# Unread matrix products in TensorE's holes, and a later place for part of a combine

## The chip, the cores and the metric

The kernel runs on one core of a Trainium2 chip. A core has five engines that run side by side, each with its own instruction queue taken in order: TensorE (PE, matrix products; its weight loads are listed as PEld), VectorE (DVE), ScalarE (ACT), GpSimd (POOL) and SyncE (SP, which here only issues DMAs). Products land in PSUM, eight banks, and are copied out by VectorE or ScalarE. The metric is the device time of one launch in microseconds (us), the median of three runs.

## The reference

Two layers on x of shape (2, 1024, 256), all float32. Layer 0: an adapter with layer norm and an RWKV-like recurrence, then a conditional feed-forward `cond2` whose output goes into a mixture of experts. Layer 1: a sparse attention `cond`, a windowed attention with side blocks, an adapter and a feed-forward. The change touches the part from `cond2` to the end of the sparse attention:

```python
h  = gelu(x @ W1 + b1); c2 = concat(h @ W2 + b2, h @ We[idx] + be)   # hidden width 1024
probs = softmax(c2 @ Wg); vals, idx = top_k(probs, 2)                # 8 experts
keep  = (one_hot == 1) & (position_in_expert < 512)                  # first choices first
x = x + sum_e combine[:, e] * (gelu(c2 @ W1[e] + b1[e]) @ W2[e] + b2[e])
Q, K, V = x @ Wq.T + bq, x @ Wk.T + bk, x @ Wv.T + bv                # 16 heads of 16
s = (Q K^T) / 4 at 32 gathered keys of each query; out = softmax(s) V @ Wo.T + bo
```

The keys that a query gathers are counted per key, and the logarithm of the count is added to dense scores over the first 256 keys, which is the same sum.

## The kernel before

The residual `x` stays in SBUF, channels on partitions, as two halves of 128 channels by 2048 tokens. The program is written with a tile framework: it finds the dependences between tiles, sets the semaphores, and orders each engine's instructions when the kernel is built, by program order as a priority and by its own costs. An instruction that is ready in that plan may be issued ahead of one written earlier.

**`cond2_0` and `Route`.** Tokens are taken in five chunks of 4, 4, 4, 3 and 1 blocks of 128 (`C2CK`). Of each chunk, eight hidden slices are made (line 671, Gelu at 674), then two halves of the output (line 680, copied out at 687). `choose` then makes router scores and the two chosen experts of each token. `place` counts tokens per expert with small products against a triangle and ones (lines 800 and 804), makes each token's slot (`si`, line 820) and issues one indirect DMA per block and choice from POOL (line 823), which scatters the token's row into a DRAM table `xs` by expert. The placing of chunk n-1 stands behind the hidden slices of chunk n, so that it has something to hide behind; that of chunk 3 stands behind the first output half of chunk 4, and that of chunk 4 at the end. `finish` makes the combine weights `cw` (softmax from line 863, Exp at 864) and, from a count over all tokens (line 841, copied at 843), the mask `k.more`.

**`moe`.** Eight experts, 512 slots each. For each one, two tables are loaded (`xe`, `more`, line 963; for expert 0 in four pieces), merged on VectorE (line 967), turned by eight 128x128 transposes on TensorE into two banks `pt` (line 982), one for each half of the channels, and copied by ScalarE to `xt` (line 983). 16 products of 512 columns follow (line 988, Gelu at 991), then 32 of 256 columns (line 996), bias on VectorE (line 999), and an indirect DMA back to `ys` from POOL (line 1000). A float32 product is two instructions in the trace, a transpose is one. Beside the first four experts VectorE counts keys (line 918), 32 instructions for each of eight query blocks.

**`combine` and `cond1_near`.** `combine` loads the two expert rows of each token for four chunks of 512 tokens (line 1029) and returns, for each chunk, three steps: `weighed` (VectorE scales and adds, lines 1038 and 1039) and two `add` steps (four transposes at line 1045, an addition to `x` at 1046). `cond1_project` gives a list of steps for one batch row: queries in four products of 512 tokens, keys, values. Before the middle attention begins, chunks 0 and 1, the whole projection of row 0, and the `weighed` steps of chunks 2 and 3 are done. Then 32 items follow (row, pair of query blocks, group of four heads): `scores` (line 1229), `weights` in two halves (VectorE adds the log counts and finds the maximum, line 1245; ScalarE's Exp at 1255), `turn` (transposes at 1264, copies at 1268), `values` (line 1292). Three items are in work at a time. What is still missing, the rest of the combine, row 1's projection and later each item's division (lines 1164 to 1176) and the output products (line 1191), waits in a first-in first-out list `later`. Each item takes one step from it ahead of `values`, and a second one behind `weights` if more than four wait. All of them share one PSUM bank. What is left in the list after the last item is run off at the end.

## Time and profile before

| | us |
|---|---|
| median of three runs | 1513.05 |
| the three runs | 1504.31, 1513.05, 1513.1 |
| the profiled execution | 1505.63 |
| its span, first to last instruction | 1503.6 |
| TensorE busy in the span | 1418.2 |
| VectorE busy | 875.4 |
| ScalarE busy | 682.6 |
| GpSimd busy | 207.4 |
| mean granted TensorE clock | 0.962 of full speed |

The page gives for each engine its busy time; busy TensorE is modelled and pipelined, so 94% is not 94% of its peak. PEclk is the clock that the throttle granted to TensorE, as a share of full speed. In the timeline, a row is a run of equal instructions: start, time, engine, line, operation, out<-in, count, and in brackets how long the engine sat idle before it and what ended that. The stretches that this document speaks of, in us from the span's start: routing to 402, the experts from 402 to 642, the combine and the projections to 669, the middle attention to 860, and the windowed attention and the last feed-forward behind it.

### The profile page before, as it was taken

How to read it: one execution, taken by the hardware profiler on the slowest of the kernel's cores; microseconds unless marked ns; L12 is line 12 of the kernel's file. 1: busy time of each engine (PE TensorE's matmuls, PEld its weight loads, DVE VectorE, ACT ScalarE, POOL GpSimd, SP SyncE). 2: the span in 40 equal slices, each digit the busy share in tenths (PEclk: the TensorE clock that was granted, in tenths of full speed). 3: DMA queues.
4: the chain of work that ended last, by engine and by line, in shares of the span. 5: the costliest groups of instructions: out<-in, count | busy, mean ns of one | idle time of the engine just before them, and what ended most of it. 6: DMA issues, size and time to landing. Idle time of an engine off the chain costs nothing. (4 is left out here: it accounts for less than half of the span.)

```text
span 1503.6 us, 27351 instructions
## 1 busy us (share of the span) xinstructions
PE 1418.2 (94%) x10788; PEld 966.2 (64%) x10788; DVE 875.4 (58%) x2775; ACT 682.6 (45%) x1683; POOL 207.4 (14%) x165
## 2 busy tenths in 40 slices
PE   6998889999699999979999999999999999999998
PEld 3446876445466766745666545788886457878866
DVE  5455643111599911067887703887883247778764
ACT  3433332322222123127888621765674337656733
POOL 3343620022311811100000000000001000000011
PEclk9899688999799999989999999999999999999999
DMA  9500004201433342030000010000000000000001
GB/s 309 189 1 3 4 9 165 108 30 38 128 118 128 119 153 71 21 119 2 2 1 2 29 56 0 2 2 2 2 2 1 0 0 2 2 1 2 2 14 44
DMA packets 42758, 70.77 MB, mean 47 GB/s; under 512 B 7168, under 2 KB 35840, under 8 KB 39552
## 3 DMA queue, kind: packets, MB, share of 16 engines
q1 hardware_dynamic: 36576, 57.12, 11.3%
q0 software_dynamic: 3072, 8.65, 1.6%
q10 hardware_dynamic: 2976, 3.18, 0.7%
q8 instruction: 87, 1.43, 0.4%
q14 instruction: 47, 0.39, 0.1%
HBM read 45.09 MB, written 23.86 MB: 46 GB/s over the span
## 5 line engine op out<-in xcount | busy, mean ns | idle before, releaser
L1643 ACT ACTIVATE pe<-pe,nm 128x320 f32<-128x320 f32 x256 | 141.8, 555 | 131.2 <-DVE nm L1633 131.0
L1633 DVE CUSTOM_DVE_ANT_0 pe<-ps,wbs 128x320 f32<-128x320 f32 x256 | 118.6, 487 | 6.1 <-PE ps L1627 1.8
L1255 ACT ACTIVATE pe<-pe,nm 128x256 f32<-128x256 f32 x256 | 110.5, 498 | 19.6 <-DVE nm L1245 19.5
L988 PE MATMUL ph<-xt,w 128*128 128x512 f32 x256 | 114.0, 603 | 2.2 <-ACT xt L983 2.2
L1623 PE MATMUL ps<-kT,qT 64*128 64x384 f32 (+1 forms) x512 | 110.2, 498 | 3.3 <-DVE qT L1597 2.8
L996 PE MATMUL po<-w,h 128*128 128x256 f32 x512 | 111.8, 379 | 0.0
L996 PEld LDWEIGHTS po<-w,h 128*128 128x128 f32 x512 | 97.3, 190 | 16.6 <-issue 3.8
L1245 DVE CUSTOM_DVE_ANT_0 pe<-ps,lc 128x256 f32<-128x256 f32 x256 | 94.1, 417 | 19.1 <-PE ps L1229 18.3
L1692 PE MATMUL py<-ptt,v 128*64 128x128 f32 x1408 | 103.6, 277 | 0.1
L918 DVE SCALAR_TENSOR_TENSOR lc<-iok,idx,lc 128x256 f32<-128x256 f32 x248 | 100.1, 479 | 0.0
L988 PEld LDWEIGHTS ph<-xt,w 128*128 128x128 f32 x256 | 48.6, 193 | 62.2 <-issue 55.6
L1000 POOL DMA_INDIRECT ys<-ye,row x32 | 60.8, 1899 | 182.3 <-DVE ye L999 162.8
L1692 PEld LDWEIGHTS py<-ptt,v 128*64 128x64 f32 x1408 | 78.6, 137 | 11.3 <-issue 8.3
L1665 PE MATMUL pt<-ident,pe 128*128 128x128 f32 x512 | 79.8, 282 | 1.9 <-DVE pe L1651 0.9
L1264 PE MATMUL ptp<-ident,pe 128*128 128x128 f32 x512 | 73.0, 280 | 3.7 <-DVE pt L1268 3.7
L991 ACT ACTIVATE h<-ph,vecs 128x512 f32<-128x512 f32 x64 | 44.0, 687 | 69.2 <-PE ph L988 69.2
L1264 PEld LDWEIGHTS ptp<-ident,pe 128*128 128x128 f32 x512 | 55.3, 141 | 31.0 <-ACT pe L1255 14.8
L1652 ACT ACTIVATE pe<-pe,rd 128x320 f32<-128x320 f32 x128 | 70.7, 557 | 8.9 <-DVE rd L1650 8.9
L1627 PEld LDWEIGHTS ps<-sk,qT 64*128 64x128 f32 x512 | 50.9, 187 | 26.2 <-issue 0.3
L1672 DVE TENSOR_TENSOR ptt<-pt,tri 128x512 f32<-128x512 f32 x96 | 65.0, 677 | 0.0
L1665 PEld LDWEIGHTS pt<-ident,pe 128*128 128x128 f32 x512 | 56.1, 140 | 10.9 <-issue 2.0
L999 DVE TENSOR_TENSOR ye<-po,b 128x256 f32<-128x256 f32 x32 | 13.5, 422 | 79.5 <-PE po L996 79.5
(368 smaller groups left out, 2784.0 us busy)
## 6 DMA issues: line engine op xcount, KB each, us to landing
w<-in_mw SPq DMA_DIRECT2D x16, 1024.0 KB, 5.2
xs<-z SPq DMA_DIRECT2D x8, 1088.0 KB, 11.7
ys<-z SPq DMA_DIRECT2D x4, 1024.0 KB, 11.4
xe<-xs SPq DMA_DIRECT2D x7, 544.0 KB, 7.0
more<-xs SPq DMA_DIRECT2D x7, 544.0 KB, 4.1
out_x<-o SPq DMA_DIRECT2D x8, 256.0 KB, 2.2
x<-in_xT SPq DMA_DIRECT2D x3, 512.0 KB, 6.4
wa<-in_wa SPq DMA_DIRECT2D x1, 1536.0 KB, 8.1
```

The costliest lines, as they stand in the source:

```text
L918: nc.vector.scalar_tensor_tensor(n, key, k.idx[:, qb, j : j + 1], n, ALU.is_equal, ALU.add)
L988: nc.tensor.matmul(ph, lhsT=w1[:, c, m * P : (m + 1) * P], rhs=xt[:, c, :], start=c == 0, stop=c == 1)
L996: nc.tensor.matmul(po, lhsT=h[:, m, j * P : (j + 1) * P], rhs=w2[:, m, :], start=m == 0, stop=m == 7)
L1245: nc.vector.tensor_tensor_reduce(out=pe[:, j, :], in0=it["ps"][i][:, j, :], in1=k.lc[:, q0 + j, :], scale=-1.0, scalar=3.0e38, op0=ALU.add ...
L1255: nc.scalar.activation(pe[:, j, :], pe[:, j, :], AF.Exp, bias=nm, scale=-1.0)
L1264: nc.tensor.transpose(ptp[:, kb, j, :], it["pe"][i][:, j, kb * P : (kb + 1) * P], k.ident)
L1623: nc.tensor.matmul(ps[:, i, keys[i]], lhsT=qs[i], rhs=kT[hp, m + pair, k0 : k0 + nk], start=True, stop=True)
L1633: nc.vector.tensor_tensor_reduce(out=pe[:, i], in0=ps[:, i, used[i]], in1=wbs[:, 0 if n == 0 else 3 if n == NB - 1 else 1 + i, (1 - i) * G ...
L1643: nc.scalar.activation(pe[:, i], pe[:, i], AF.Exp, bias=nm[:, i : i + 1], scale=-1.0, accum_out=den[:, i : i + 1])
L1652: nc.scalar.activation(pe[:, 1], pe[:, 1], AF.Copy, scale=rd[:, 1:2])
L1665: nc.tensor.transpose(pt[1 - j if i and inner(n) else j][:, 2 * pair + i, :], pe[:, at : at + P], k.ident)
L1692: nc.tensor.matmul(py[64 * i : 64 * i + 64, (m + pair) % 4, :], lhsT=keys[:, hs], rhs=it["pts"][:, pair, :] if j == 3 else it["pt"][:, j, ...
```

## The change

Three helpers of order and filling come in. `behind` adds an edge of order without a semaphore, so that one instruction is issued behind another on its engine. `spin` issues products of the identity with itself into a bank that nobody reads, each behind the one before, 512 columns unless told otherwise. `k.step`, `k.placed` and `k.added` remember the instruction to stand behind.

- `cond2_0`: `place(ch - 1)` stands ahead of both output halves for every chunk, so for the last one too.
- `finish`: its first VectorE instructions, the copy of the count and the subtraction ahead of Exp, stand behind the last slot of `place`.
- `moe`: seven spins for expert 0 behind the count; both `pt` banks are taken at once and the transposes go block by block, for every expert; with expert 0 a spin of 256 columns stands behind each of the first three blocks.
- `combine`: the scaling of chunks 1 to 3 stands behind the last addition or the last reduction of `weights` written before it; chunk 0's transposes stand behind the spins.
- `cond1_project`: for the near form, values come ahead of the queries of the row's second half.
- `cond1_near`: ahead of the items there are eight spins, chunk 0's three steps, two spins, and five projection steps (queries and keys of the first half, values). The list begins with chunk 1, the two other query steps of row 0, chunks 2 and 3 with their scalings, and row 1's projection. Two spins of 256 columns stand in the run-off at the end.

```diff
+def behind(k, ins, other):
+    how = mybir.DependencyInfo(mybir.DependencyClass.NoSync, mybir.DependencyReason.DATA)
+    k.tc.add_manual_dep(ins.ins, other.ins.name, how, reason="order")
+    return ins
+
+def spin(k, bank, other, count, n=4):
+    for _ in range(count):
+        rhs = k.ident.unsqueeze(1).to_broadcast([P, n, P])
+        out = bank[:, 0 : n * P].rearrange("p (n c) -> p n c", c=P)
+        other = behind(k, k.nc.tensor.matmul(out, lhsT=k.ident, rhs=rhs, start=True, stop=True), other)
+    return other
...
-            if 0 < ch < end:
+            if ch:
                 place(ch - 1)
...
-                if ch == end and c == 0:
-                    place(ch - 1)
             choose(ch)
-        place(end)
+        place(ch)
...
-        nc.vector.tensor_add(self.si[:, bs], q, at)
+        k.placed = nc.vector.tensor_add(self.si[:, bs], q, at)
...
-        nc.vector.tensor_copy(c1, pc[:, 0, 0])
+        behind(k, nc.vector.tensor_copy(c1, pc[:, 0, 0]), k.placed)
...
-        nc.vector.tensor_sub(ex, self.L, bc(self.top))
+        behind(k, nc.vector.tensor_sub(ex, self.L, bc(self.top)), k.placed)
...
+            pts = [pp.tile([P, CAP], F32, name="pt") for _ in range(2)]
+            if e == 0:
+                warm = pp.tile([P, 2 * C], F32, name="po", bufs=4)
+                k.step = spin(k, warm, k.step, 7)
+            for j in range(4):
+                for c in range(2):
+                    t = nc.tensor.transpose(pts[c][:, j * P : (j + 1) * P], xe[:, j, c * P : (c + 1) * P], k.ident)
+                    if e == 0:
+                        k.step = behind(k, t, k.step)
+                if e == 0 and j < 3:
+                    k.step = spin(k, warm, k.step, 1, 2)
             for c in range(2):
-                pt = pp.tile([P, CAP], F32, name="pt")
-                for j in range(4):
-                    nc.tensor.transpose(pt[:, j * P : (j + 1) * P], xe[:, j, c * P : (c + 1) * P], k.ident)
-                nc.scalar.copy(xt[:, c, :], pt)
+                nc.scalar.copy(xt[:, c, :], pts[c])
...
-            nc.vector.tensor_scalar_mul(o, o, k.cw[:, 0, blk : blk + 1])
+            first = nc.vector.tensor_scalar_mul(o, o, k.cw[:, 0, blk : blk + 1])
+            if ch:
+                behind(k, first, k.added)
...
-    return steps + [lambda bank, j=j: values(bank, j) for j in range(0, keys // P, 2)]
+    n = 4 if keys < S else len(steps)
+    return steps[:n] + [lambda bank, j=j: values(bank, j) for j in range(0, keys // P, 2)] + steps[n:]
...
-            for step in sums[0] + sums[1] + project[0] + [sums[2].pop(0), sums[3].pop(0)]:
+            warm = wp.tile([P, CK], F32, name="warm")
+            k.step = spin(k, warm, k.step, 8)
+            for step in sums[0]:
+                step(lambda shape: pp.tile(shape, F32, name="pb"))
+            k.step = spin(k, warm, k.step, 2)
+            for step in project[0][:5]:
                 step(lambda shape: pp.tile(shape, F32, name="pb"))
...
-            second = [lambda step=step: step(bank) for step in sums[2] + sums[3] + project[1]]
+            second = [lambda step=step: step(bank) for step in sums[1] + project[0][5:] + sums[2] + sums[3] + project[1]]
...
-            for step in later:
+            warm = None
+            for i, step in enumerate(later):
                 step()
+                if len(later) - i in (5, 3):
+                    warm = warm or bank([P, CK])
+                    k.step = spin(k, warm, k.step, 1, 2)
```

More of the change, by code (lines that the diff above doesn't have):

```diff
@@ L660, in cond2_0 @@
     ):
-        end = len(C2CK) - 1
         for ch, (b0, nb) in enumerate(C2CK):
@@ L840, in finish @@
         pc = self.pp.tile([P, CK // P, 2, E], F32, name="pc")
-        nc.tensor.matmul(pc[:, 0, 0], lhsT=k.ones, rhs=self.run[:, 0, 0], start=True, stop=True)
+        k.step = nc.tensor.matmul(pc[:, 0, 0], lhsT=k.ones, rhs=self.run[:, 0, 0], start=True, stop=True)
         c1 = rt.tile([P, E], F32, name="c1")
-        nc.vector.tensor_copy(c1, pc[:, 0, 0])
+        behind(k, nc.vector.tensor_copy(c1, pc[:, 0, 0]), k.placed)
         k.more = rp.tile([P, E, CAP // P], F32, name="more")
@@ L995, in moe @@
                 for m in range(8):
-                    nc.tensor.matmul(
+                    k.step = nc.tensor.matmul(
                         po, lhsT=h[:, m, j * P : (j + 1) * P], rhs=w2[:, m, :], start=m == 0, stop=m == 7
@@ L1044, in add @@
         for j in range(4):
-            nc.tensor.transpose(po[:, j * P : (j + 1) * P], gs[ch][0][:, j, c * P : (c + 1) * P], k.ident)
-        nc.vector.tensor_add(x[:, c, ts], x[:, c, ts], po)
+            t = nc.tensor.transpose(po[:, j * P : (j + 1) * P], gs[ch][0][:, j, c * P : (c + 1) * P], k.ident)
+            if ch == 0:
+                k.step = behind(k, t, k.step)
+        k.added = nc.vector.tensor_add(x[:, c, ts], x[:, c, ts], po)
     return [
@@ L1163, in divide @@
         for g in range(4):
-            nc.tensor.transpose(pa[:, g, :], aU[g], k.ident)
+            k.step = nc.tensor.transpose(pa[:, g, :], aU[g], k.ident)
         p4 = pa.rearrange("p g (r d) -> p (g r) d", d=32)
@@ L1173, in back @@
         for c in range(2):
-            nc.tensor.transpose(pb[:, c, :], a2[:, c * P : (c + 1) * P], k.ident)
+            k.step = nc.tensor.transpose(pb[:, c, :], a2[:, c * P : (c + 1) * P], k.ident)
         for c in range(2):
@@ L1214, in cond1_near @@
             its += [dict(at=(b, q0, g), qT=qT, kT=kT, v=v, aT=aT) for q0 in range(0, 8, 2) for g in range(4)]
-        with tiles(tc, name="l1a", bufs=6, space=PSUM) as pp:
-            for step in sums[0] + sums[1] + project[0] + [sums[2].pop(0), sums[3].pop(0)]:
+        with tiles(tc, name="l1a", bufs=6, space=PSUM) as pp, tiles(tc, name="l1w", bufs=1, space=PSUM) as wp:
+            warm = wp.tile([P, CK], F32, name="warm")
[4 more added lines that the diff above has]
+            for step in project[0][:5]:
                 step(lambda shape: pp.tile(shape, F32, name="pb"))
@@ L1244, in weights @@
                         nm = sp.tile([P, 1], F32, name="nm", bufs=4)
-                        nc.vector.tensor_tensor_reduce(
+                        k.added = nc.vector.tensor_tensor_reduce(
                             out=pe[:, j, :],
```

## The prediction

> **What bounds the kernel now.** I read the page first: 1503.6 us of span in a profiled execution of 1505.63 us, so 2.0 us lie around the span. TensorE is busy for 94% and leads the chain that ended last (PE 28%, DVE 10%, ACT 3%). The row PEclk is 9 or 8 nearly everywhere, so only short pieces of the run can win from a faster clock. Then I asked for busy time and granted clock in stretches of 3.41 us around the two holes of TensorE that the change fills (393 to 414, 643 to 660) and the end of the middle attention (858 to 864). The columns are the stretch, its length, busy time of PE, PEld, DVE, ACT and POOL, granted clock, DMA share and GB/s.

> ```profile
> 396.77:400.18 3.41, 0.00 (x0) 0.00 (x0) 3.31 (x26) 0.00 (x0) 2.50 (x4) 0.50 0.28 106
> ...
> 407.01:410.42 3.41, 2.18 (x7) 1.01 (x7) 2.46 (x9) 1.03 (x2) 0.00 (x0) 0.50 0.88 187
> 410.42:413.83 3.41, 3.41 (x5) 1.35 (x5) 3.31 (x10) 1.32 (x2) 0.00 (x0) 0.50 1.11 367
> ...
> 649.36:652.77 3.41, 2.37 (x8) 1.30 (x8) 2.08 (x6) 0.00 (x0) 0.00 (x0) 0.50 1.09 353
> ...
> 857.58:860.99 3.41, 2.08 (x15) 1.30 (x12) 2.30 (x9) 0.37 (x1) 0.00 (x0) 1.00 0.02 5
> 860.99:864.40 3.41, 3.41 (x5) 1.35 (x4) 2.57 (x5) 0.19 (x1) 0.00 (x0) 0.50 0.00 0
> ```

> The clock changes at the edges of such stretches. It falls to 0.50 after one with 2.08 us of products and comes back after one that is full. With 2.37 or 2.18 us at the low clock it doesn't come back. What the low clock costs is small: half of the 3.8 us in which expert 0's products ran slow (410.03 to 413.83), some 1.8 us in front of the attention, 1.7 us behind it.

> **Part 1, routing.** Now `place(3)` stands behind eight pairs of output products; this is the timeline.

> ```profile
> 386.10 1.95 PE L680 MATMUL po<-h,c2w 128*128 128x128 f32 x16
> 387.89 0.32 PE L800 MATMUL pc<-oh,tri 128*128 128x48 f32 x2
> ...
> 389.86 0.17 DVE L820 TENSOR_TENSOR si<-q,at 128x6 int32<-128x6 f32 x1
> ...
> 390.77 0.96 POOL L823 DMA_INDIRECT xs<-ct,si  x1 [8.65 <-issue]
> ...
> 399.72 0.96 POOL L823 DMA_INDIRECT xs<-ct,si  x1 [0.30 <-issue]
> ...
> 402.29 1.76 SPq L963 DMA_DIRECT2D xe<-xs  x4
> ```

> In front of both halves its counting starts at 386.10, 1.79 us earlier, and so does POOL's run of scatters, one each 1.27 us. The last two need the last block's `si`. Now it ends at 396.68; without `ex` (0.2) and the copy of `c1` with its wait for TensorE (0.26) in front it is ready at about 396.1, and POOL takes it some 0.75 us later, at 396.85 instead of 398.45. So the loads of `xe` start 1.6 us earlier (bounds 1.0 and 1.8). `finish` loses nothing: `ex` and its chain, 3.6 us of VectorE, then end near 401.3, before the first `xe` is there (405.07 less 1.6). POOL has no other work there, and SP's loads only wait for the scatters.

> **Part 2, the seven spins.** One is a 128x512 product, two instructions of 0.43 us at full clock (L988's step) and of 0.86 at half. From 396.0 they run 12.0 us if the clock stays low and about 8.1 if it is back at 400.18, so to 404.1, when the first `xe` is there. In 403.59:407.01 the rest of them, three short spins of 0.43 and six transposes (0.27 each) give 2.6 us of products, above the 2.08 that was followed by a fall. So I take it that expert 0 starts at full clock: 2.0 us of its 32 instructions (15.7 us instead of 13.66 at 0.427) are saved. [...]

> With 1.6 and 2.0 and 0.2 for faster transposes TensorE is 3.8 us ahead at expert 0's end, but VectorE, which counts keys (0.39 us x 32, twice per expert) without a break, is only 1.9 ahead (1.6, and 0.3 of a wait at 429.0 that goes). It ended expert 1's `xe` at 438.85, now 436.95; the last two transposes and a copy take 1.0 more, so L988 starts at 437.95 instead of 440.82: 2.9 us of the 3.8 arrive.

> **Part 3, the transposes of all experts.** The order changes from channel half by channel half to block by block. Where TensorE ends one expert and goes on, the copy to `xt` waits for the fourth transpose; afterwards for the seventh.

> ```profile
> 439.55 1.04 PE L982 MATMUL pt<-ident,xe 128*128 128x128 f32 x8
> ...
> 440.18 1.07 ACT L983 COPY xt<-pt 128x512 f32<-128x512 f32 x2 [13.56 <-PE pt L982]
> ...
> 440.82 1.98 PE L988 MATMUL ph<-xt,w 128*128 128x512 f32 x4 [0.24 <-ACT xt L983]
> ```

> Eight take 1.04 us, so they follow each other by 0.11, and three are 0.33 us of TensorE's path in each of experts 2 to 6: 1.65 us given back (0 if they are issued early, as half of expert 7's were at 589.26, bounded above by 1.0 for expert 7 besides). At 642 us the sum is -1.25.

> **Part 4, in front of the attention.** Now the second chunk's first scaling waits on VectorE for its DMA, with the first chunk's additions behind it.

> ```profile
> 653.31 0.62 DVE L1038 TENSOR_SCALAR g<-g,cw 128x256 f32<-128x256 f32 x2 [1.79 <-DMA g<-ys]
> 653.84 1.28 DVE L1046 TENSOR_TENSOR x<-x,pb 128x512 f32<-128x512 f32 x2
> ...
> 656.06 1.91 PE L1112 MATMUL pb<-x,w1c 128*128 128x512 f32 x2
> ...
> 668.88 1.93 PE L1229 MATMUL ps<-kT,qT 32*128 32x256 f32 x16
> ```

> Afterwards the first chunk's sum is ready at about 653.25. Two spins behind its transposes (652.2) hold TensorE till 653.9. The five projections that stay in front are 4 + 4 + 4 + 4 + 8 instructions of 0.43, 0.215, 0.43, 0.215 and 0.215, 6.85 us: scores at 660.8 instead of 668.88, -8.1. The eight spins run from 642.05 to 648.9, and till 652.2 there are only eight transposes, less than the 2.08 that let the clock fall; so I take 1.7 us off: -6.4.

> **Part 5, what the attention takes over.** Three scalings of a chunk (w, VectorE: half of one, two L1038 and two L1039, takes 1.32 us, so 2.64), two additions (a) and two query products (q) join its list. Each of 32 items takes one step before `values`, and a second if more than four wait.

> ```profile
> 700.82 1.88 PE L1112 MATMUL pa<-x,w1c 128*128 128x512 f32 x4
> 702.64 1.07 PE L1292 MATMUL po<-pt,v 128*32 128x256 f32 x16
> 704.25 1.98 PE L1112 MATMUL pa<-x,w1c 128*128 128x512 f32 x4 [0.54 <-DVE qT L1123]
> 706.07 1.04 PE L1264 MATMUL ptp<-ident,pe 128*128 128x128 f32 x8
> ```

> From one item's scores to the next TensorE needs 3.97 us bare, 1.82 for q, 0.97 for k, 1.83 for v or an output product (O), 0.53 for a, and 0.61 where the second step waits for the one bank. VectorE needs 8 x 0.345 + 2 x 0.60, plus 0.60 for a, 0.67 for q, 2.64 for w. The rows bear it out: an item with q,k is 7.37, q,q 8.22, a,a 5.92, O,O 8.83, two of the small steps of a division 5.63 to 5.72, one of them 4.95. In the new order:
> - Items 0 to 6 have w; a; a,q; q,w; a,a; w,a; a,q: 6.0, 5.04, 6.93, 7.27, 5.92, 7.20, 6.93, together 45.3 instead of 45.1.
> - Items 7 to 9 have k,q; k,v; q,q: 7.37, 7.38, 8.22 instead of 4.96, 4.95, 5.63, so +7.4.
> - Later the queue drains: more second steps (+0.76 each at 11, 12 and 18, +0.68 at 26), and O,O splits (items 13 to 15: -3.11 + 1.75 + 1.05; 20 to 22: -0.36 - 2.13 + 1.05). Sum +1.2.

> Together +8.8. The bounds are 4.7, TensorE's moved work alone with all of VectorE's in its idle time (2.57 us in an item of 7.37), and 14, if no w hides.

> **Part 6, the end.** Two half spins (0.43) fall into TensorE's waits of 0.70 and 0.63 at 859.26 and 860.66. They lift 857.58:860.99 from 2.08 to 2.9 us busy, and the output products that took 3.51 us there instead of 1.88 run at full clock: -1.7 (0 where the clock would not have fallen).

> **The sum.** -1.25 - 6.4 + 8.8 - 1.7 = -0.5 us, so 1505.1 for the profiled execution. The runs were 1504.31, 1513.05 and 1513.1; no row tells why they differ, so I lay the sum on the mean of all four executions, 1509.0: **1508.5 us**. About 1% (15 us) can be told from no change here.

> **Rivals.**
> - The scalings hide. For it: VectorE idles 1.66 + 0.91 us in each q,k item. Against: in items 0 and 1 it has no gap, and two of the three stand beside additions or in the first item. Attention +4.7, front -8.1 with the clock held: -1.25 - 8.1 + 4.7 - 1.7 = -6.4, 1502.6 on the mean.
> - Slower: VectorE becomes the attention's bound in items 0 to 5. A w behind the last of an item's reductions delays the copy from `ptp`, of which there are two banks, and so the transposes of the next item; nothing hides, and +14 is its price: -1.25 - 6.4 + 14 - 1.7 = +4.7, 1513.7. It decides once the stage grows by over 9.4 us. Against it: TensorE alone needs 6.4 us in q,w.
> - The spins do not hold the clock (the change does not do what it says): expert 0 slow (+2.0 against the sum, less 0.4 that VectorE held back anyway), the end slow (+1.7): 1.6 + 1.7 - 0.5 = +2.8, 1511.8.

> **How the numbers follow.** Forecast 0.42 (its own range -3 to +2.5 us, 1506 to 1511.5 on the mean), hidden scalings 0.25, VectorE as bound 0.15, clock not held 0.18. Over the cases the change is worth -6.4 to +4.7 us. Laid on runs between 1504.3 and 1513.1, with a little left out at both ends, the range is 1499 to 1518. No case reaches 1%; only with the scatter of the runs can one: faster 0.06, same 0.88, slower 0.06.

> **What would show it.** Part 1: POOL's last scatter at about 398.1. Part 2: clock 1.00 where L988 begins, its 32 instructions in 13.7 us. Part 3: 0.5 to 0.6 us instead of 0.24 before L988. Part 4: the first L1229 at 659 to 663. Part 5: L1229 to the last L1292 takes 197 us instead of 188, items 7 to 9 over 7 us each. Part 6: L1191 at 1.9 us. The prediction is wrong if VectorE's new work is issued elsewhere than where it is written, if the experts' pace is set by VectorE more than the 0.7 us of slack says, or if the runs scatter further.

## The result

The changed kernel is slower: 1519.68 us (median of 12 runs, 1510.99 to 1523.35) against 1506.21 us for the kernel before (12 runs, 1498.54 to 1513.10) on the same chip. The ratio is 1.0079, with a 95% interval of 1.0058 to 1.0099, that is +11.9 us (8.7 to 14.9); the two medians lie 13.5 us apart, the means 12.2. The forecast was no change (-0.5 us). The profiled execution took 1520.6 us, its span 1518.7 us. TensorE is busy for 1438.1 us instead of 1418.2, and 44 instructions of the 10832 are the unread products. VectorE's busy time is the same (875.6 instead of 875.4), and the mean granted clock rose from 0.962 to 0.969. So TensorE had more clock, and the time was lost elsewhere.

Line numbers are now those of the changed kernel: the expert products are L1009 and L1017 (before L988 and L996), the transposes L998, the scores L1260, the reductions L1276, the output products L1217. First the holes, in stretches of 3.41 us (length, busy time of PE, PEld, DVE, ACT and POOL, granted clock, DMA share, GB/s).

```profile
397.60:401.01 3.41, 2.03 (x7) 1.86 (x8) 2.25 (x18) 0.25 (x1) 2.20 (x4) 0.50 0.28 100
401.01:404.42 3.41, 3.41 (x5) 1.34 (x5) 3.14 (x22) 0.06 (x1) 1.82 (x2) 0.50 0.28 105
404.43:407.84 3.41, 3.41 (x9) 1.50 (x9) 1.15 (x6) 0.00 (x0) 0.00 (x0) 1.00 0.66 197
407.84:411.25 3.41, 3.17 (x17) 1.94 (x15) 2.25 (x9) 0.00 (x0) 0.00 (x0) 1.00 1.01 303
653.61:657.02 3.41, 1.64 (x6) 0.47 (x4) 2.90 (x8) 0.00 (x0) 0.00 (x0) 1.00 1.09 361
657.03:660.43 3.40, 3.40 (x8) 2.07 (x9) 1.37 (x2) 0.00 (x0) 0.00 (x0) 0.50 1.09 349
```

The spins fill 401.01 to 407.84, the clock is back at 404.43 and stays; expert 0's 32 instructions take 14.0 us instead of 15.9. In front of the attention the clock still fell once, at 657.03, after a stretch with 1.64 us of products. The next three fences are the timelines of SP's queue and of VectorE beside it, and the same rows of the kernel before.

```profile
404.73 3.07 SPq L976 DMA_DIRECT2D xe<-xs  x5
407.93 0.43 SPq L914 DMA_DIRECT2D ii<-in_idx  x1
408.46 0.55 SPq L916 DMA_DIRECT2D mm<-in_idxm  x1
```

```profile
413.05 0.29 DVE L919 CAST idx<-ii 128x256 f32<-128x256 int32 x1 [1.88 <-DMA ii<-in_idx]
...
414.50 0.62 DVE L929 TENSOR_SCALAR lc<-iok,idx 128x256 f32<-128x256 f32 x2
```

```profile
405.02 0.39 SPq L901 DMA_DIRECT2D ii<-in_idx  x1
...
409.21 0.29 DVE L906 CAST idx<-ii 128x256 f32<-128x256 int32 x1
...
410.59 0.62 DVE L916 TENSOR_SCALAR lc<-iok,idx 128x256 f32<-128x256 f32 x2
```

SP issues five loads of `xe` ahead of the key list `ii`, where the kernel before had four: the fifth is expert 1's, 544 KB. VectorE waits 1.88 us for `ii`, where it did not wait before. So it begins to count keys 24.2 us behind the last chunk's hidden products, against 24.3 before, though the loads of expert 0's rows were issued 1.6 us earlier. TensorE's timeline at experts 1 and 2 shows what follows, and the price of the new order of the transposes:

```profile
442.71 0.44 PE L998 MATMUL pt<-ident,xe 128*128 128x128 f32 x2 [0.30 <-DVE xe L980]
443.71 6.71 PE L1009 MATMUL ph<-xt,w 128*128 128x512 f32 x15 [0.57 <-ACT xt L1004]
...
471.36 1.04 PE L998 MATMUL pt<-ident,xe 128*128 128x128 f32 x8
473.02 1.55 PE L1009 MATMUL ph<-xt,w 128*128 128x512 f32 x3 [0.62 <-ACT xt L1004]
```

Expert 1 waits for VectorE's merges; expert 2 shows the wait of 0.62 us for ScalarE's copy, which was 0.29 there in the kernel before. In the attention, VectorE's timeline in item 0 and TensorE's in item 7:

```profile
673.53 0.69 DVE L1299 COPY pt<-ptp 128x512 f32<-128x512 f32 x1 [1.12 <-PE ptp L1295]
674.14 0.41 DVE L1276 CUSTOM_DVE_ANT_0 pe<-ps,lc 128x256 f32<-128x256 f32 x1
674.48 0.08 DVE L1276 DVE_READ_ACCUMULATOR2_ANT nm<- 128x1 f32 x1
674.48 0.61 DVE L1059 TENSOR_SCALAR g<-g,cw 128x256 f32<-128x256 f32 x2
675.00 0.88 DVE L1062 SCALAR_TENSOR_TENSOR g<-g,cw,g 128x256 f32<-128x256 f32 x2
675.80 0.61 DVE L1059 TENSOR_SCALAR g<-g,cw 128x256 f32<-128x256 f32 x2
676.32 0.88 DVE L1062 SCALAR_TENSOR_TENSOR g<-g,cw,g 128x256 f32<-128x256 f32 x2
677.11 0.42 DVE L1276 CUSTOM_DVE_ANT_0 pe<-ps,lc 128x256 f32<-128x256 f32 x1
```

```profile
716.22 1.03 PE L1137 MATMUL pa<-x,w1c 128*128 128x256 f32 x4
717.18 1.07 PE L1323 MATMUL po<-pt,v 128*32 128x256 f32 x16
718.18 0.66 PE L1295 MATMUL ptp<-ident,pe 128*128 128x128 f32 x4
719.90 1.98 PE L1137 MATMUL pa<-x,w1c 128*128 128x512 f32 x4 [1.06 <-ACT kT L1154]
```

Item 0's last reduction (674.14) stands behind a copy that waits 1.12 us for TensorE. Behind it stands the scaling of the second chunk, 2.63 us long, and item 1's first reduction (677.11) behind that: from item 0's first reduction to item 1's it is 7.20 us instead of 3.96. In the kernel before only the copy stood between the two reductions:

```profile
673.44 0.42 DVE L1245 CUSTOM_DVE_ANT_0 pe<-ps,lc 128x256 f32<-128x256 f32 x1
...
673.78 0.69 DVE L1268 COPY pt<-ptp 128x512 f32<-128x512 f32 x1
674.39 0.41 DVE L1245 CUSTOM_DVE_ANT_0 pe<-ps,lc 128x256 f32<-128x256 f32 x1
```

In items 7 and 8 a key product (L1137, 256 columns) now goes ahead of a query product (item 7) or of the values (item 8), and the one bank comes free after ScalarE's copy, 1.06 us of wait where the query copy on VectorE cost 0.54 to 0.61. Last, the end of the attention on TensorE:

```profile
871.43 1.98 PE L1217 MATMUL pa<-aT,w1c 128*128 128x512 f32 x4 [0.20 <-DVE aT L1202]
873.25 1.88 PE L1217 MATMUL ps<-aT,w1c 128*128 128x512 f32 x4
876.00 1.53 PE L1559 MATMUL pq<-c,w1ak 128*128 128x512 f32 x3 [0.87 <-ACT c L1218]
```

The output products run at full clock (1.9 us each, as forecast), but the next attention's first product waits 0.87 us for ScalarE's copy of the last one. In the kernel before (its second profile, `before_again`, where the clock did not fall) it followed at once:

```profile
862.90 1.88 PE L1191 MATMUL pa<-aT,w1c 128*128 128x512 f32 x4
864.62 2.74 PE L1524 MATMUL pq<-c,w1ak 128*128 128x512 f32 x6
```

In this pair of profiles the stages from routing to the end of the attention account for +6.1 us; +4.05 stand ahead of 390 us and +4.9 behind 880, where the program is the same instruction for instruction. So beside the question of which part costs what there was a second one: is that remainder scatter, or does the change cause it? Theory A: the stages' own costs add up and the rest is scatter. Theory B: the change costs something systematic in stages that it doesn't touch.

### The profile page after: what moved, and what is told of

It reads as the page before. It is cut to its first block, busy times and chain, and to the rows that moved or that the text cites. A ratio compares the mean times of both kernels' runs of the same rounds, so it can differ in the third digit from the quotient of the medians.

```text
span 1518.7 us, 27437 instructions
## 1 busy us (share of the span) xinstructions
PE 1438.1 (95%) x10832; PEld 972.4 (64%) x10832; DVE 875.6 (58%) x2775; ACT 684.2 (45%) x1683; POOL 186.3 (12%) x165
## 3 DMA queue, kind: packets, MB, share of 16 engines
q1 hardware_dynamic: 36576, 57.12, 11.3%
q0 software_dynamic: 3072, 8.65, 1.6%
## 5 line engine op out<-in xcount | busy, mean ns | idle before, releaser
L1286 ACT ACTIVATE pe<-pe,nm 128x256 f32<-128x256 f32 x256 | 110.5, 498 | 28.4 <-DVE nm L1276 28.4
L1009 PE MATMUL ph<-xt,w 128*128 128x512 f32 x256 | 112.2, 595 | 4.9 <-ACT xt L1004 4.9
L1017 PE MATMUL po<-w,h 128*128 128x256 f32 x512 | 111.8, 379 | 0.0
L1017 PEld LDWEIGHTS po<-w,h 128*128 128x128 f32 x512 | 97.3, 190 | 16.6 <-issue 3.8
L1276 DVE CUSTOM_DVE_ANT_0 pe<-ps,lc 128x256 f32<-128x256 f32 x256 | 93.7, 418 | 22.5 <-PE ps L1260 22.4
L1009 PEld LDWEIGHTS ph<-xt,w 128*128 128x128 f32 x256 | 47.9, 190 | 63.7 <-issue 55.0
L1727 PEld LDWEIGHTS py<-ptt,v 128*64 128x64 f32 x1408 | 78.7, 137 | 11.3 <-issue 8.3
L1295 PEld LDWEIGHTS ptp<-ident,pe 128*128 128x128 f32 x512 | 55.7, 141 | 30.6 <-ACT pe L1286 13.7
L1662 PEld LDWEIGHTS ps<-sk,qT 64*128 64x128 f32 x512 | 50.9, 187 | 26.2 <-issue 0.3
L1021 POOL DMA_INDIRECT ys<-ye,row x32 | 40.2, 1256 | 205.8 <-DVE ye L1020 184.2
L1749 PE MATMUL ps<-yT,w1ao 128*128 128x256 f32 x256 | 59.0, 385 | 0.9 <-ACT yT L1739 0.3
## 6 DMA issues: line engine op xcount, KB each, us to landing
xs<-z SPq DMA_DIRECT2D x8, 1088.0 KB, 11.9
```

Of the source, the lines that this page charges most:

```text
L1009: nc.tensor.matmul(ph, lhsT=w1[:, c, m * P : (m + 1) * P], rhs=xt[:, c, :], start=c == 0, stop=c == 1)
L1017: k.step = nc.tensor.matmul(po, lhsT=h[:, m, j * P : (j + 1) * P], rhs=w2[:, m, :], start=m == 0, stop=m == 7)
L1286: nc.scalar.activation(pe[:, j, :], pe[:, j, :], AF.Exp, bias=nm, scale=-1.0)
L1295: nc.tensor.transpose(ptp[:, kb, j, :], it["pe"][i][:, j, kb * P : (kb + 1) * P], k.ident)
L1727: nc.tensor.matmul(py[64 * i : 64 * i + 64, (m + pair) % 4, :], lhsT=keys[:, hs], rhs=it["pts"][:, pair, :] if j == 3 else it["pt"][:, j, ...
L1749: nc.tensor.matmul(po[:, c, 0 : 2 * P], lhsT=wo[:, m, c * P : (c + 1) * P], rhs=yT[:, m, :], start=m == 0, stop=m == 7)
```

## The experiments

**Both kernels again, and the change in two halves.** `after_again` and `before_again` are unchanged copies. `e_routing` has routing and experts changed, `e_attention` has front, attention and end changed:

```diff
 e_routing: the changed kernel, with the front, list and end of before
-            warm = wp.tile([P, CK], F32, name="warm")
-            k.step = spin(k, warm, k.step, 8)
...
+            for step in sums[0] + sums[1] + project[0] + [sums[2].pop(0), sums[3].pop(0)]:
...
+            second = [lambda step=step: step(bank) for step in sums[2] + sums[3] + project[1]]
 e_attention: the changed kernel, with the placing and the transposes of before
+            if 0 < ch < len(C2CK) - 1:
...
-            pts = [pp.tile([P, CAP], F32, name="pt") for _ in range(2)]
```

> The changed kernel once more, for a second profile of it. Theory A (the stages add up: experts +1.3 us, front -5.9, middle attention +11.3, its end -0.6, together about +6, and the rest of the 12 us measured was the scatter of the clock's low stretches over the first 390 us and the last 650): 5 to 9 us over the kernel before, the same stage times within 0.5 us, but other sums ahead of 390 us and behind 870 us. Theory B (the change costs something systematic in the stages whose program it does not touch): again 10 to 14 us over, with some 4 us more ahead of 390 us and some 3 more behind 870 us.

> The kernel before once more, as a second profile of it and as a measure of what two sets of runs of one kernel differ by. Both theories: within 1.5 us of the runs beside it. By A its profile, too, has the stretches ahead of 390 us and behind 870 us up to 4 us away from the first profile's; by B they are within 1 us.

> Only routing and experts are changed (places, spins for expert 0, transposes block by block); front and attention are those of the kernel before. Theory A: the experts end 1.3 us later, front and attention as before, together +1 to +2 us. Theory B (something outside the attention carries half of the 12 us, whichever part is changed): +4 us or more. My prediction had -1.25 for these parts.

> Only the front, the attention's list and its end are changed (spins there included); routing and experts are those of the kernel before. Theory A: front -5.9, attention +11.3, end -0.6: +4 to +6 us. Theory B: +8 us or more. My prediction had +0.7 for these parts (-6.4 + 8.8 - 1.7).

Against runs of the kernel before beside them (median 1508.30): `after_again` 1522.75, ratio 1.0083 (1.0050 to 1.0116); `before_again` 1509.46, 1.0018 (1.0000 to 1.0036), so by the ratio an unchanged copy came out 2.7 us away, further than the 1.5 expected; `e_routing` 1513.08, 1.0032 (1.0014 to 1.0050), +4.8 us; `e_attention` 1521.72, 1.0101 (1.0070 to 1.0132), +15.2 us. By stages `e_routing` has +1.2 us at the end of the experts and +0.9 in front of the attention, where its clock was low for 17.07 us instead of 13.65; the rest is as before. So both halves are slower, and the attention is the larger. `e_attention`'s stages in its profile add up to some +9 us, below its measured interval of 10.6 to 19.9; its profiled execution was the fastest of its six. By the totals `after_again` (+12.5 us), `e_routing` and `e_attention` all lie where theory B had them, but with the 2.7 us of the unchanged copy beside them, and +2.1 by its own stages, `e_routing` alone decides nothing.

The second profile of the changed kernel (span 1527.1) brought what the first did not show. These are stretches at the beginning of its attention:

```profile
672.43:675.83 3.40, 1.82 (x20) 1.09 (x19) 1.23 (x7) 2.63 (x4) 0.00 (x0) 1.00 0.00 0
675.84:679.25 3.41, 3.41 (x11) 1.69 (x10) 1.26 (x8) 2.13 (x6) 0.00 (x0) 0.50 0.02 5
679.26:682.66 3.40, 3.40 (x14) 2.59 (x13) 2.90 (x10) 0.99 (x2) 0.00 (x0) 0.50 0.00 0
682.67:686.07 3.40, 3.40 (x13) 2.18 (x12) 3.40 (x16) 2.27 (x6) 0.00 (x0) 0.50 0.00 0
686.08:689.49 3.41, 3.41 (x25) 2.21 (x26) 1.96 (x8) 1.73 (x5) 0.00 (x0) 1.00 0.00 0
```

While TensorE waits at the beginning of the attention it has 1.82 us of products in a stretch, the clock falls, and it comes back only after three full stretches. The attention took 193.77 us there, 190.12 in the first profile. With the eight profiles of the changed list (with its spins) taken together, the clock fell there in four, for 6.8 or 10.2 us, which cost 2.3 to 3.7 us; in the five with the list of the kernel before it never did. The same happened once at expert 1, where TensorE waits for VectorE: in `after_again` expert 1 took 31.00 us instead of 29.31.

**The transposes.** By halves for experts 1 to 7:

```diff
-            pts = [pp.tile([P, CAP], F32, name="pt") for _ in range(2)]
+            pts = [pp.tile([P, CAP], F32, name="pt") for _ in range(2)] if e == 0 else []
...
+                else:
+                    pt = pp.tile([P, CAP], F32, name="pt")
+                    for j in range(4):
+                        nc.tensor.transpose(pt[:, j * P : (j + 1) * P], xe[:, j, c * P : (c + 1) * P], k.ident)
```

> The changed kernel, but for experts 1 to 7 the transposes go by channel halves as in the kernel before. If block by block costs what I priced (0.33 us in each of experts 2 to 6, about 0.8 in expert 7): the stretch from expert 0's first product to the end of expert 7 shrinks from 235.4 to about 232.8 us, the wait ahead of the first products of an expert falls from 0.5 to 0.24, and the whole is 2 to 3 us below the changed kernel. Rival (the wait only moves to another place): 235 us, no change.

1517.72 us, ratio 1.0053 (1.0035 to 1.0072), some 4 us below the changed kernel. An expert takes 28.98 us again instead of 29.31, expert 7's beginning 28.53 instead of 29.31. TensorE at expert 2:

```profile
473.30 1.04 PE L1008 MATMUL pt<-ident,xe 128*128 128x128 f32 x8
474.63 3.70 PE L1014 MATMUL ph<-xt,w 128*128 128x512 f32 x8 [0.29 <-ACT xt L1009]
```

The stretch of the experts is 233.47 us instead of 235.42. The price of block by block is as I had it, 0.33 for each of experts 2 to 6, with 0.78 for expert 7; expert 1 came 0.5 later in this profile, because of the key list.

**The key list's place on SP.** One edge of order, behind the lists:

```diff
-        nc.sync.dma_start(out=mm, in_=ins["idxm"].rearrange("(q p) j -> p q j", p=P))
+        k.counts = nc.sync.dma_start(out=mm, in_=ins["idxm"].rearrange("(q p) j -> p q j", p=P))
...
+                    if e == 1 and t is xe:
+                        behind(k, load, k.counts)
```

> The changed kernel with one edge of order more: on SP the load of expert 1's rows stands behind the two loads of the key lists. If VectorE's late start with the lists took the rest of the 2.9 us that I expected at expert 1: the counting begins 1.5 to 2 us earlier, expert 1's first product comes 31.0 to 31.3 us behind expert 0's instead of 31.75 less what the transposes take, TensorE's hole there closes to under 2 us, and the stretch of the experts falls from 235.4 to about 233.7. Rival (VectorE's pace there is set by the chain of the combine weights): no change.

1520.96 us, ratio 1.0077 (1.0055 to 1.0098): no change, and the experiment didn't test what it was to test. With expert 1's `xe` held back, its other table, `more`, also 544 KB, was issued ahead of `ii` (at 406.89, `ii` at 407.37), and the counting began 24.0 us behind the last chunk's hidden products, against 24.2. Expert 1's first product came 31.02 us behind expert 0's, as expected, but it did so in `e_scaled` too, which has no such edge. `best_experts` below holds both tables back.

**The scalings.** Chunks 1 to 3 back in front, behind chunk 0's additions:

```diff
-            for step in project[0][:5]:
+            for step in project[0][:5] + [sums[n].pop(0) for n in (1, 2, 3)]:
```

> The changed kernel with the scalings of chunks 1, 2 and 3 (VectorE alone, 2.64 us each) back in front of the attention, behind chunk 0's additions. Theory 1 (the scalings delay the items that take them): the attention, from item 0's first reduction to item 31's, falls from 190 to 184 (within 1.5), the front grows by 0 to 3 us. Theory 2 (the growth is TensorE's moved products and the waits for the one bank): the attention stays above 188 us.

1509.76 us, ratio 1.0010 (0.9991 to 1.0030): the largest effect of a single edit, some 10 us below the changed kernel. The attention takes 183.50 us, the front 21.24. So theory 1 holds: 4.6 us of the attention's growth are TensorE's moved work (my lower bound was 4.7), 6.6 come with the three scalings. The rest of the 10 us lies in falls of the clock at the attention's beginning, of which this profile has none, and in the last stage (570.81 us instead of 573.3 on the mean). Item 0 is back at 3.95 us. The scalings cost next to nothing in front (20.8 to 21.2 us with the clock held), since VectorE runs them while TensorE projects:

```profile
666.65 0.61 DVE L1059 TENSOR_SCALAR g<-g,cw 128x256 f32<-128x256 f32 x2
667.17 0.88 DVE L1062 SCALAR_TENSOR_TENSOR g<-g,cw,g 128x256 f32<-128x256 f32 x2
667.97 0.42 DVE L1276 CUSTOM_DVE_ANT_0 pe<-ps,lc 128x256 f32<-128x256 f32 x1
```

**No unread products.** The loop in `spin` runs over nothing; order and places stay:

```diff
-    for _ in range(count):
+    for _ in range(0):
```

> The changed kernel without its unread products; order and places stay. If they do what I took them to do: the low clock lasts from about 397 to 418, expert 0's 32 instructions take 15.7 us instead of 13.7, of which expert 1 sees 0 to 0.5 because VectorE is late there; the front gains 0.75 (the two spins ahead of the projections) and loses 1.7 to the low clock; the end loses or gains up to 1.7. Together 0 to +3 us over the changed kernel. Rival (the spins cost more than they save): 1 to 3 us below it.

1523.90 us, ratio 1.0093 (1.0071 to 1.0116), not told apart from the changed kernel. Expert 0's 32 instructions took 16.75 us instead of 14.0, and expert 1 began 0.6 to 1.4 us later; the front took 21.98, within the 20.8 to 22.6 of the profiles with spins; the end took 15.97, the same. What the spins bring is about 1 us at the experts (258.3 us to their end, against 257.6 on the mean), and nothing seen in front or at the end.

**Mended versions.** `best_experts` keeps the placing and expert 0's spins, with the front and list of before, transposes by halves, and both of expert 1's loads behind the lists. `best_spins` adds eight spins in front of the attention. `mended` is the changed kernel with the scalings in front, the halves, both loads behind the lists, and at the end the unread products written to the bank that the next step takes:

```diff
+                    if e == 1:
+                        behind(k, load, k.counts)
...
-                    warm = warm or bank([P, CK])
-                    k.step = spin(k, warm, k.step, 1, 2)
+                    k.step = spin(k, bank([P, CK]), k.step, 1, 2)
+                    spare.insert(0, spare.pop())
```

> Routing, the spins of expert 0 and nothing else of the change: front, attention and end are those of the kernel before, transposes of experts 1 to 7 by halves, and both of expert 1's loads (rows and later rows) stand behind the key lists on SP. Theory of the queue (544 KB ahead of the lists on SP made VectorE late): counting begins 1.5 to 2 us earlier than in the changed kernel, counted from the end of the last chunk's hidden slices (22.4 to 22.9 us behind it instead of 24.2 to 24.9), expert 1's first product at 51.7 to 52.3 instead of 53.3 to 54.1 and 54.3 to 54.6 in the kernel before, and the experts end 252.8 to 253.6 us behind that point instead of 257.1 (changed) and 255.5 to 255.8 (before): 2 to 3 us below the kernel before. Rival (the DMA engines are full there, order does not matter): expert 1 at 53.3 or later and 254.3, 1 to 1.5 us below the kernel before.

> The same with eight unread products in front of the attention as well, in the order of the kernel before. If holding the clock is worth 1.5 to 2 us there: front 26.5 to 27 instead of 28.4 us, whole 4 to 5 us below the kernel before. Rival (the clock falls anyway in the 3 us between the spins and the projections): front 28 to 29 us, 2 to 3 us below.

> The changed kernel with the four things mended that the runs point to: scalings of chunks 1 to 3 back in front, transposes of experts 1 to 7 by halves, both of expert 1's loads behind the key lists, and the unread products at the end written to the bank that the next step takes, so that the banks of the run-off stand as in the kernel before. By the stages: experts' end -1.2 to -2.7 against the kernel before, front -7.1, attention +4.7, end (item 31 to the next attention's first product) 14.9 instead of 16.0: together 4 to 6 us below the kernel before, less up to 3 us if the last stage's low stretch (4.96 to 8.3 us of low clock, against 0.96 to 4.8) comes with it. Theory B (something in the shifted program costs more outside these stages): no faster than the kernel before. If the end stays at 16.0, the bank is not its cause.

Against 1507.19 us (the kernel before, the median of its 27 runs under 1515 us): `best_experts` 1503.71, ratio 0.9974 (0.9955 to 0.9993); `best_spins` 1505.25, 0.9973 (0.9956 to 0.9991); `mended` 1503.76, 0.9978 (0.9957 to 0.9999). All three come out 3 to 4 us below the kernel before, a little more than the unchanged copy was away, and can't be ranked; the experts' stage, 2.8 to 3.6 us shorter in all three, bears it out. Expected were 2 to 3 us for `best_experts` and 4 to 6 for `mended`. The queue's theory holds, and with more than was expected of it. These are SP, VectorE and TensorE in `best_experts`:

```profile
404.71 1.75 SPq L976 DMA_DIRECT2D xe<-xs  x4
407.55 0.39 SPq L914 DMA_DIRECT2D ii<-in_idx  x1
...
408.73 0.89 SPq L976 DMA_DIRECT2D xe<-xs  x1
```

```profile
412.29 0.61 DVE L929 TENSOR_SCALAR lc<-iok,idx 128x256 f32<-128x256 f32 x2
```

```profile
439.37 1.55 PE L1010 MATMUL pt<-ident,xe 128*128 128x128 f32 x8
441.15 2.41 PE L1016 MATMUL ph<-xt,w 128*128 128x512 f32 x5 [0.24 <-ACT xt L1011]
```

Counted from the end of the last chunk's hidden products, the counting begins at 22.0 us (after: 24.2), expert 1 at 50.9 (after: 53.4, before: 54.6), and the experts end at 252.1 (after: 257.1, before: 255.8). In `best_spins` the rival holds: the low clock in front is halved (6.83 us instead of 13.65), but the front takes 28.61 us, against 28.99; the whole doesn't tell 2 to 3 us from 4 to 5. In `mended` the front is 22.49, the attention 183.44, the end 15.06.

**The remainder.** Two kernels add nothing but delay ahead of the last output products (three or six unread products of 256 columns more), and `e_endbank` is the changed kernel with the bank edit of `mended` alone:

```diff
 e_shift3 (e_shift6: 7 instead of 4)
-                    k.step = spin(k, warm, k.step, 1, 2)
+                    k.step = spin(k, warm, k.step, 1 if len(later) - i == 5 else 4, 2)
```

> The changed kernel, but the two unread products at the end are written to the bank that the next step takes anyway, so that the banks of the run-off stand as in the kernel before. If the bank makes the 0.87 us wait ahead of the next attention: the stretch from item 31 to that attention's first product is 14.9 to 15.1 us instead of 15.97. Theory of the grid (the low stretch behind 870 us depends only on where the clock's windows of 3.41 us stand when the last stage begins): the stage then begins 1.0 us earlier against the windows, its time falls from 573.7 to 570 to 571, the whole is 3 to 5 us below the changed kernel. Rival (the last stage's extra 3 us have a cause of their own in the changed program): 573.7 again, the whole 1 us below.

> The changed kernel with three more unread products of 256 columns (0.43 us each, 0.2 of which fall into a wait) ahead of the last output products: 1.1 us of pure delay. Theory of the grid: the last stage begins 1.1 us later against the windows (1.9 to 2.6 us behind a window's edge, where the profiles of other kernels had 568.8) and takes 568.8 to 570 instead of 573.7: with the delay the whole is 2 to 4 us FASTER than the changed kernel. Rival: 573.7 and 1.1 us slower.

> The same with six more, 2.4 us of delay. Theory of the grid: the last stage begins 3.2 to 3.9 us (so up to 0.5 past the next edge), where other profiles had 570.3 to 570.9: the whole within 1.5 us of the changed kernel although 2.4 us were put in. Rival: 573.7 and 2.4 us slower.

Against 1509.80 us: `e_endbank` 1520.28, ratio 1.0071 (1.0049 to 1.0093); `e_shift3` 1524.41, 1.0098 (1.0075 to 1.0120); `e_shift6` 1524.32, 1.0108 (1.0076 to 1.0139). The end of `e_endbank` takes 15.06 us, so the bank is the cause of the 0.87 us wait:

```profile
869.94 1.96 PE L1217 MATMUL ps<-aT,w1c 128*128 128x512 f32 x4 [0.35 <-DVE aT L1202]
871.73 1.88 PE L1217 MATMUL pa<-aT,w1c 128*128 128x512 f32 x4
873.45 2.74 PE L1558 MATMUL pq<-c,w1ak 128*128 128x512 f32 x6
```

The times did not come out as the grid theory had them. `e_endbank` is 1 us below the changed kernel, as its rival had it, and its last stage took 572.18 us, between the 570 to 571 of the theory and the 573.7 of the rival. In `e_shift3` the clock had also fallen at the attention's beginning (193.84 us), so the last stage stood elsewhere on the grid than I had reckoned, and took 573.99 us. In `e_shift6` it began near an edge, as expected, and took 572.07, neither the 570.3 to 570.9 of the theory nor the 573.7 of the rival. All three are explained by laying all sixteen profiles side by side. All clock changes of a profile lie on one grid of 3.413 us (in `before` 0.81 us behind the span's start, in `after` 1.65). Take the place on that grid at which the windowed attention's first scores begin, and the time that the last stage's product behind its one thin spot (some 515 us later) is late against the first profile of before:

| place on the grid, us | late by, us | kernels |
|---|---|---|
| 0.02 to 0.23 | 1.6 to 1.8 | e_shift6, best_experts, best_spins |
| 0.75 to 0.84 | 1.8 to 2.0 | e_scaled, before_again, e_attention |
| 1.03 to 1.53 | 3.3 to 3.5 | after_again, e_nospin, e_halves, after, e_shift3, e_iifirst |
| 2.16 to 2.90 | 0.0 | before, mended |
| 3.06 to 3.30 | 1.8 to 2.1 | e_routing, e_endbank |

In four of the five rows kernels with the old and the new list stand together, and `e_shift6`, `e_attention` and `e_endbank`, which have the new list with its scalings, lose what the old ones beside them lose, within 0.3 us. So the loss goes with the place and not with the list. In the row with 3.3 to 3.5, though, no profile of the old list stands. At the thin spot VectorE is full and TensorE has some 2 us of products in a stretch; the changed kernel's stretch shows it, and what follows:

```profile
1452.32:1455.73 3.41, 2.06 (x6) 0.47 (x5) 3.41 (x8) 0.69 (x1) 0.00 (x0) 1.00 0.00 0
1455.73:1462.56 6.83, 6.83 (x8) 2.45 (x9) 6.33 (x10) 1.66 (x2) 3.03 (x2) 0.50 0.00 0
```

The rest of the last stage's difference stands at the very end. From the start of TensorE's last product to the end of the span it is 5.33 to 5.53 us in the seven profiles in which VectorE's queue has 2995 instructions in its records, and 6.83 to 7.42 in the nine (the changed list with its scalings) in which it has 2990; the five are EVENT_SEMAPHORE, and the other 2781 are the same in number. What is late there is VectorE's last DRAIN, which the trace has 4.8 to 5.0 us behind the start of that product, or 6.5 to 7.1. The edit of `e_scaled` takes it away (5.46 us). What the DRAIN waits for isn't settled. In all nine a packet of 8 KB on the queue that the view lists as q14, `instruction`, stands 1.7 to 1.9 us ahead of it, when the outputs are out (in the changed kernel at 1516.6 us); that the DRAIN waits for it is a guess.

The stages ahead of 390 us took 382.69 to 392.58 us over the sixteen profiles, 390.28 and 392.13 of it with the old front and list. So the +4.05 us there lie within the scatter, as theory A had it; the last stage took 572.1 to 574.0 us in all nine profiles with the scalings in the list and 568.8 to 570.9 in the five of the old list, as theory B had it.

## Why the prediction was wrong

The account, as means over all profiles in which a stage has the one or the other program unmended (in the last row `e_nospin`, `e_shift3`, `e_shift6` and `e_endbank` are in):

| stage | before | changed | difference | forecast |
|---|---|---|---|---|
| hidden products to the experts' end | 255.7 (3) | 257.6 (7) | +1.9 | -1.25 |
| to item 0's first reduction | 28.7 (4) | 21.7 (8) | -7.1 | -6.4 |
| to item 31's first reduction | 178.9 (5) | 191.8 (8) | +12.9 | +8.8 |
| to the windowed attention's first product | 15.3 (5) | 16.0 (5) | +0.7 | -1.7 |
| its first scores to the end | 570.2 (5) | 573.3 (9) | +3.1 | 0 |

The sum is +11.5 us, against +11.9 (8.7 to 14.9) measured. The stretch ahead of it is left out: 388.4 us on the mean with the old list (5 profiles), 389.6 with the new one (9), a small difference against the scatter of 10 us.

- **Part 1** held. The last two scatters were issued 1.6 us earlier (400.91 and 402.17, less the 4.05 of scatter ahead of them), and no other engine lost by the place.
- **Part 2, "2.9 us of the 3.8 arrive", failed.** The clock was held. Whether the transposes that I counted in do anything for it, no run tells: in 407.84 to 411.25 (3.17 us of products) the end of the seven spins, three half spins and the transposes together kept it at 1.00, and the spins alone may have been enough. What failed was the 1.9 us by which I had VectorE ahead. I moved the loads of `xe` and not the load of the key list behind them, and took SP's order from the trace of before; in the changed kernel 544 KB stand ahead of the list. The counting began 0.1 us later on the mean instead of 1.9 earlier, and expert 1 began 0.8 us earlier instead of 2.9. With both tables held back it began 2.7 to 3.6 us earlier, so the step was right but for the queue.
- **Part 3** held in kind. Five times 0.33, and 0.78 for expert 7, inside the bound that I had given and not taken.
- **Part 4** held: -7.1 instead of -6.4, though in half of the profiles the clock still fell there (22.3 to 22.6 us instead of 20.8 to 21.2).
- **Part 5, "+8.8", is where the largest part was lost.** Without falls of the clock the attention grew by 11.3. The term that failed is that of the scalings: above the 4.7 of TensorE's moved work I had 4.1 us for them, and `e_scaled` shows that they bring 6.6. By items, of the 2.5 us too much items 7 and 8 have 1.3 (8.03 instead of 7.37), the items behind item 9 have 0.8 (+2.0 instead of +1.2), and items 0 to 6 together 0.3: item 0 took 7.20 instead of 6.0, but items 1 and 6 gave 0.9 back. I had counted a scaling as VectorE's time added to an item, with what gap there was taken off. In VectorE's timeline it stands ahead of all of the next item's reductions (2.63 us between item 0 and item 1), and in item 0 nothing hid it. The scalings also move the steps behind them, so that k,q takes the place of q,k, and I had k,q at the price of q,k: the copy that frees the bank is another engine's (ScalarE's, 1.06 us of wait instead of 0.54 to 0.61). The mean has 1.6 more, because the clock falls at the attention's beginning in half of the profiles, where TensorE waits. The rival "VectorE becomes the bound in items 0 to 5", which I gave 0.15, is near in number (+14, measured +12.9), and the growth is over its mark of 9.4 us. Its mechanism is shown in part only. VectorE is busy without a break in items 1, 3 and 5, but items 3 and 5 took 7.25 and 7.19 us, as the forecast had them (7.27 and 7.20), and of the 12.9 us 1.6 are falls of the clock. So its nearness is partly luck. The rival "the scalings hide" is right only where they have a hole: `e_scaled` has its 4.7.
- **Part 6, "-1.7", failed.** The output products do run at full clock. But four of five profiles of the old program had them so, too, and took 14.9 us; the 16.6 that I priced was the one with a fall. And asking for a bank for the unread products turned the banks of the run-off by one, which put 0.87 us of wait ahead of the next attention.
- **What had no term.** +3.1 us in a stage that the change doesn't touch: in the profiled executions 1.5 go with its place on the clock's grid and 1.6 with VectorE's last DRAIN. I had the falls of the clock as part of single holes, not as something that a shift of everything behind them changes. And I took 2.08 us of products in a stretch as the mark below which the clock falls. The runs have no such mark: the changed kernel kept the full clock after 1.91 us (667.26 to 670.67) and 2.04 us (438.56 to 441.97), and the kernel before fell after 2.55 us (86.15 to 89.56), `e_attention` after 2.68 (666.07 to 669.48).
- The runs scatter further than the four times of before had shown: 1498.5 to 1513.1 over 12 runs, 14.6 us instead of 8.8.

Left open: why the loads were ordered otherwise on SP, how often the changed kernel's last stage stands in the worst place (only profiled executions show it), and the rest of `e_attention`'s +15.2 us.

## What to carry to other kernels

Work that is moved off one engine's path costs what it delays on the engine that it lands on: look between which two instructions it stands, not only at the idle time of the item (item 0 here: 7.20 us instead of 3.96). When a transfer is moved, list the queue behind it anew from the changed order, since one large load ahead of a small one took back most of the gain (expert 1 began 0.8 us earlier instead of 2.9). An unread product is not free of resources either, a bank that it asks for may be the next stage's (0.87 us of wait here); and a gain of a few us in a kernel whose clock changes on a grid that starts elsewhere in each profile has to be told from where the grid put the rest (0 to 3.5 us here).
